# Attention and mixture of experts in one program: expert blocks in the attention's buffers, two of them between its last steps, and another order of a step's pieces

## The chip, the cores and the metric

The kernel runs on one core of one Trainium2 chip. The core has five engines that run side by side and in order, each its own list of instructions: TensorE (PE, with its weight loads PEld), VectorE (DVE), ScalarE (ACT), GpSimd (POOL) and SyncE (SP), which here issues most DMAs. The metric is the device time in microseconds of the slowest core, of which there is one; smaller is better.

## The reference

```python
x = hidden                                            # (4, 1024, 256), float32
x = x + layernorm(attention(layernorm(x)))
x = x + layernorm(experts(layernorm(x)))

def attention(x):                                     # 16 heads of 16
    q, k, v = heads(x @ Wq + bq), heads(x @ Wk + bk), heads(x @ Wv + bv)
    pos_k = heads(rel_embeddings @ Wk + bk)           # 128 buckets
    scores = (q @ k.T + take(q @ pos_k.T, c2p_pos) + take(k @ pos_k.T, p2c_pos).T) / sqrt(48)
    out = softmax(scores) @ v @ Wo + bo + x
    return layernorm(out) * ln_scale + ln_bias

def experts(x):                                       # 8 experts, 256 -> 1024 -> 256
    e = argmax(softmax(x @ Wr + br))
    out = 0
    for i in range(8):                                # an expert sees zeros for the rows of others
        out = out + relu((x * (e == i)) @ W1[i] + b1[i]) @ W2[i] + b2[i]
    return out
```

What an expert gives for a row of zeros is the same for all rows, so the kernel adds it once as a constant (`dh`), and each row needs only its own expert.

## The kernel before, in words

Everything is float32. All work after the setup is issued under a manual schedule: an engine's instructions run in the order in which the program's functions are called, and waits come only from data and from buffers that must come free. So the order of calls in the loop over steps is the schedule.

**Attention.** There are 128 steps `u`, one for each batch element (4), group of four heads (4) and tile of 128 queries (8), and 4 more to finish. Step u does the first pass of its tile: `turn_x` and `first_x` put position terms and scores near the diagonal into four PSUM banks, `near_x` (L523, L527) drains them on VectorE into a `kept` tile and takes maxima, `first_y` (L540, L547, L548) does the same for the other keys, and GpSimd takes the maxima off `kept` (L552). `tables(u+3)` (L435, L441) computes position tables three steps ahead, which go to HBM and come back skewed (`skewed`) into `qpos` and `kpos` tiles; `mend` (L460) repairs their edges. Beside it runs the second pass over the four tiles before, a block of 512 queries, two key tiles in a step: `turn_near` (L576) and `keys` (L598) build transposed scores, ScalarE takes exp (L605) into a `pt` tile, and `sums` (L615) multiplies it by the values into the one bank `pv`. After the eighth key tile ScalarE copies `pv` to `sv`, and `divide` (L634, L639) in the next step turns it round. There are seven other banks (`unit`), handed out in turn. A step with s = u mod 4 equal to 0 also has `maxima` and `add_maxima` (L558, L565), which bring the row maxima of the block's four tiles into q.

**The queue.** When the last head group of 512 rows is divided, `finish` puts the rest of these rows' work into a list, two row tiles an item: `turn` (L690), `out_proj` (L703, L707), `scale` (L716, L717), `scaled`, `residual` (L90, L732), `again`, `logits0`, `logits` (L756), `logits2` (L767), `choose` and `place`, then the scatter of row numbers into the experts' lists, which goes into a second list, `late`. `slot()` takes one item of the first list, `one_late()` one of the second. A step has three slots, the four steps behind the last tile five.

**Experts.** Rows are worked in 39 blocks of 128 rows of one expert. 17 of them hold only rows of the first three batch elements and are planned before the last one is done. A block is `gather` (an indirect DMA), `measure` and `center` (layernorm, L90), `turn_in` (L965, L967), `layer1` (L977; relu L985 on ScalarE and L987 on VectorE in turn), `layer2` (L994, L997) and `close` (layernorm, residual, scatter to the output, L1007). `weights(i)` loads 2 MB for a block through SP's queue (L936, L938), two blocks ahead, into pools of their own that are opened when the attention's pools are closed. The loop over blocks calls, in this order: center(i+1), layer1(i), close(i-1), slot, weights(i+2), turn_in(i+1), slot, measure(i+2), start, layer2(i), slot, slot.

Of the kernel before, what the change touches and what calls it, by code (L numbers as in the profile page):

```python
# [47 lines left out]
def tile_layer(  # L48
# [49 lines left out]
    with ExitStack() as ax:  # L98
# [267 lines left out]
        inner = ax.enter_context(ExitStack())  # L366
        qkp = inner.enter_context(tc.tile_pool(name="qkp", bufs=2))
        vp = inner.enter_context(tc.tile_pool(name="vp", bufs=NG + 1))
        ring = inner.enter_context(tc.tile_pool(name="ring", bufs=4))
        ptp = inner.enter_context(tc.tile_pool(name="ptp", bufs=2))  # L370
# [303 lines left out]
        queue, late = [], []  # L674

        def finish(b, hf):
# [6 lines left out]
            rs, keep_ = {}, {}  # L683

            def turn(t):
                pm = unit()
                for n in range(2):
                    for k in range(KC):
                        at = (n * KC + k) * P
                        nc.tensor.transpose(pm[:, at : at + P], ctx_[:, t_0 + t + n, k * P : (k + 1) * P], ident)  # L690
                cT = two.tile([P, 512], F32, name="cT", tag="sv")
                nc.scalar.copy(cT, pm)
                xr = xin.tile([P, 2, C], F32, name="xr", tag="xt")
                r0 = (b * NT + t_0 + t) * P
                nc.sync.dma_start(out=xr, in_=xrh[r0 : r0 + 2 * P, :].rearrange("(t p) c -> p t c", p=P))
                keep_[t] = cT, xr

            def out_proj(t):
                cT, xr = keep_.pop(t)
# [19 lines left out]
            def scaled(t):  # L719
# [4 lines left out]
                xt = xin.tile([P, 2, C], F32, name="xt")  # L724
                nc.sync.dma_start(out=xt, in_=x_t[b][:, t_0 + t : t_0 + t + 2, :])
                keep_[t] = xt

            def residual(t):
                xt = keep_.pop(t)
                for n in range(2):  # L730
                    normalize(o[:, t + n, :], o[:, t + n, :], agg[1], rs[1], t + n)
                nc.gpsimd.tensor_tensor(o[:, t : t + 2, :], o[:, t : t + 2, :], xt, ALU.add)  # L732
                r0 = (b * NT + t_0 + t) * P
# [44 lines left out]
            def choose():  # L778

# [35 lines left out]
            pairs = range(0, HT, 2)  # L815
            for t in pairs:
                queue.append((turn, t))
                if t:
                    queue.append((out_proj, t - 2))
            queue.append((out_proj, HT - 2))  # L820
# [13 lines left out]
            for t in range(HT):  # L834
                queue.append((late.append, (scatter, t)))
# [79 lines left out]

        live = {}

# [9 lines left out]
        def weights(i):  # L927
# [5 lines left out]
            dr = v["dr"] = e_p[0].tile([P, C], F32, name="dr", bufs=4)  # L933
            nc.sync.dma_start(out=dr, in_=dh[e].to_broadcast([P, C]))
            w1 = v["w1"] = w_p[0].tile([P, KC, FF], F32, name="w1")
            nc.sync.dma_start(out=w1, in_=w1_d[e].rearrange("o (k p) f -> p (o k) f", p=P))  # L936
            w2 = v["w2"] = w_p[0].tile([P, NFC, C], F32, name="w2")
            nc.sync.dma_start(out=w2, in_=w2_d[e].rearrange("o (f p) c -> p (o f) c", p=P))  # L938

        def gather(i):  # L940

            v = live[i]
            x = v["x"] = e_p[0].tile([P, C], F32, name="x", bufs=7)
# [11 lines left out]
        def center(i):  # L955
            v = live[i]
            xn = v["xn"] = e_p[0].tile([P, C], F32, name="xn", bufs=2)
            normalize(xn, v["x"], *v["agg"], 0)

        def turn_in(i):  # L960
# [5 lines left out]
            x2T = v["x2T"] = e_p[0].tile([P, KC, TB], F32, name="x2T", bufs=2)  # L966
            nc.scalar.copy(x2T.rearrange("p k t -> p (k t)"), pm[:, :C])  # L967

        def layer1(i):
            v = live[i]  # L970
            h = v["h"] = e_p[0].tile([P, NFC, TB], F32, name="h", bufs=2)
            for f0 in range(0, NFC, 4):
                ph = unit()
                for j in range(4):
                    f = f0 + j
                    for kc in range(KC):
                        nc.tensor.matmul(  # L977
                            ph[:, j * TB : (j + 1) * TB], lhsT=v["w1"][:, kc, f * P : (f + 1) * P], rhs=v["x2T"][:, kc, :],
                            start=(kc == 0), stop=(kc == KC - 1),
                        )  # L980
                for j in range(4):
                    f = f0 + j
                    hp, b = ph[:, j * TB : (j + 1) * TB], v["b1s"][:, f : f + 1]
                    if j % 2 == 0:
                        nc.scalar.activation(h[:, f, :], hp, AF.Relu, bias=b)  # L985
                    else:
                        nc.vector.tensor_scalar(h[:, f, :], hp, b, 0.0, ALU.add, ALU.max)  # L987

        def layer2(i):
# [3 lines left out]
            for f in range(NFC):  # L993
                nc.tensor.matmul(py, lhsT=v["h"][:, f, :], rhs=v["w2"][:, f, :], start=(f == 0), stop=(f == NFC - 1))  # L994
            agg = small.tile([P, NT, 2], F32, name="agg")
            ys = v["ys"] = e_p[0].tile([P, C], F32, name="ys", bufs=3)
# [4 lines left out]
        def close(i):  # L1001

            v = live.pop(i)
            y = e_p[0].tile([P, C], F32, name="y", bufs=4)
# [76 lines left out]

        for u in range(NU + QB):
# [3 lines left out]
            if s == 0:  # L1086
                slot()
                ahead(u, load, 0)
                if one:
                    turn_x(u)  # L1090
                if one:
                    first_x(u)
                if two_:
                    pm = maxima(blk)
                if one:
                    near_x(u, 0, 2)
# [12 lines left out]
                if tails:  # L1109
                    divide(*tails.pop(0))  # L1110
                ahead(u, prep1, 1)
                extras(u)
# [8 lines left out]
                slot()  # L1121
                if two_:
# [5 lines left out]
                if u + 1 < NU:  # L1128
                    mend(u + 1, 0)
                if one:  # L1130
                    first_y(u)
                one_late()
            else:
                if two_:
                    turn_near(*where(blk, 2 * s))
                if two_:
                    keys(blk, 2 * s)
                if one:
                    turn_x(u)
                if one:  # L1140
                    first_x(u)
                if one:
                    near_x(u, 0, GH)
                ahead(u, load, 0)
# [8 lines left out]
                slot()  # L1153
                sums(0)
                if two_:
                    turn_near(*where(blk, 2 * s + 1))
                if two_:
# [5 lines left out]
                if tails:  # L1163
                    divide(*tails.pop(0))
# [118 lines left out]
```

## Time and profile before

| what | value |
|---|---|
| time, median of 3 runs | 2078.43 us (2071.1 to 2079.08) |
| profiled execution, its own time | 2073.61 us |
| its span | 2071.9 us |
| TensorE, VectorE, ScalarE, GpSimd busy | 94%, 69%, 47%, 27% |
| HBM read and written | 316.85 and 153.83 MB |

The span runs from the first to the last instruction; the execution's own time has 1.7 us more around it. All shares and durations in the text come from that one execution. In rows of instructions, `[4.53 <-DVE xn L90]` says that the engine sat idle 4.53 us just before and what released it. TensorE's records are pipelined and their ends are modelled, so a busy TensorE need not be at its peak; a float32 matmul shows as more than one record.

### The profile page before, as it was taken

To read this page: it belongs to the slowest core of one execution; us is meant where nothing else is said; L and a number is where in the kernel's file an instruction comes from. 1 tells how busy PE (TensorE), PEld (TensorE's weight loads), DVE (VectorE), ACT (ScalarE), POOL (GpSimd) and SP (SyncE) were. 2 spreads that over 40 slices of the span, in tenths; PEclk is the share of its full clock that TensorE was granted. 3 is DMA by queue.
4 is the path that set the end of the run, shared out by engine and by line. 5 is a ranking of instruction groups with operands and counts; after the bars stand their busy time and mean duration, and the time that the engine had idled before them with its cause. 6 is when DMAs were issued, how large, how long until landed. Compare 5 with 4: busy or idle time off the path is not lost.

```text
span 2071.9 us, 43363 instructions
## 1 busy us (share of the span) xinstructions
PE 1951.6 (94%) x15727; PEld 1191.7 (58%) x15727; DVE 1431.5 (69%) x4765; ACT 965.4 (47%) x1916; POOL 569.8 (27%) x966
## 2 busy tenths in 40 slices
PE   7799999999999999999999999999999998899996
PEld 4455555555555555555555555555555555789996
DVE  5567676868677668686767686877786765665654
ACT  1245555554555555554545555545465543122221
POOL 2112212322222213222222222222322122444442
PEclk9899999999999999999999999999999998999999
DMA  5777777766566678665667786666677735799994
GB/s 153 232 253 249 252 248 245 261 216 212 184 220 210 206 229 256 214 212 188 215 208 224 230 258 214 208 196 206 213 216 215 246 118 172 236 332 347 350 337 142
DMA packets 387657, 472.60 MB, mean 228 GB/s; under 512 B 27711, under 2 KB 374931, under 8 KB 387444
## 3 DMA queue, kind: packets, MB, share of 16 engines
q1 hardware_dynamic: 382676, 460.49, 69.4%
q0 software_dynamic: 4768, 9.33, 1.5%
q8 instruction: 125, 2.05, 0.4%
q14 instruction: 88, 0.72, 0.1%
HBM read 316.85 MB, written 153.83 MB: 227 GB/s over the span
## 4 chain that ended last, share of the span: by engine, by line
PE 69%; DVE 15%; DMA 8%; issue 3%; ACT 2%; POOL 1%; SPq 0%; POOLq 0%; DVEq 0%; ACTq 0%
PE pv L615 9%; PE u L598 8%; PE u L540 7%; PE u L576 6%; PE u L491 6%; PE u L387 5%; PE u L435 5%; PE u L994 5%; PE u L507 5%; PE u L977 5%; DVE mx L547 3%; DMA shift<-stage 2%; DVE qpos L460 2%; DMA qpos<-shift 2%; DVE kept L523 2%
## 5 line engine op out<-in xcount | busy, mean ns | idle before, releaser
L605 ACT ACTIVATE pt<-u 128x512 f32<-128x512 f32 x1024 | 529.8, 608 | 268.2 <-PE u L598 262.4
L547 DVE TENSOR_REDUCE mx<-u 128x1 f32<-128x512 f32 x512 | 317.5, 682 | 197.8 <-PE u L540 197.8
L552 POOL TENSOR_SCALAR kept<-kept,m 128x384 f32<-128x384 f32 (+1 forms) x512 | 291.9, 586 | 524.5 <-DVE m L548 357.9
L441 ACT COPY stage<-u 128x512 f32<-128x512 f32 x512 | 263.1, 604 | 320.0 <-issue 179.2
L523 DVE CUSTOM_DVE_ANT_0 kept<-u,qpos 128x384 f32<-128x384 f32 (+1 forms) x512 | 263.4, 515 | 137.6 <-PE u L507 137.4
L615 PE MATMUL pv<-pt,v 128*24 128x512 f32 x2048 | 274.6, 605 | 0.0
L576 PE MATMUL u<-ident,kept 128*128 128x128 f32 x1408 | 200.7, 282 | 34.5 <-DVE mx L527 22.5
L576 PEld LDWEIGHTS u<-ident,kept 128*128 128x128 f32 x1408 | 153.0, 142 | 137.7 <-issue 39.0
L443 POOL COPY ends<-stage 128x8 f32<-128x8 f32 x128 | 26.5, 207 | 655.8 <-ACT stage L441 655.8
L491 PE MATMUL u<-ident,kpos 128*128 128x128 f32 x1408 | 194.3, 285 | 11.2 <-DMA kpos<-shift 6.3
L491 PEld LDWEIGHTS u<-ident,kpos 128*128 128x128 f32 x1408 | 155.0, 143 | 78.9 <-DVE mx L547 21.4
L460 DVE SCALAR_TENSOR_TENSOR qpos<-mask,ends,qpos 128x128 f32<-128x128 f32 x448 | 177.3, 456 | 23.8 <-DMA qpos<-shift 23.8
L985 ACT ACTIVATE h<-u,b1s 128x128 f32<-128x128 f32 x156 | 55.6, 367 | 236.7 <-issue 140.4
L527 DVE TENSOR_REDUCE mx<-u 128x1 f32<-128x128 f32 (+1 forms) x512 | 162.6, 318 | 0.0
L540 PE MATMUL u<-k_hi,q 32*128 32x512 f32 (+3 forms) x768 | 155.2, 509 | 7.2 <-ACT pt L605 5.7
L460 DVE SCALAR_TENSOR_TENSOR kpos<-mask,ends,kpos 128x128 f32<-128x128 f32 x448 | 131.9, 355 | 28.7 <-DMA kpos<-shift 28.7
L977 PEld LDWEIGHTS u<-x2T,w 128*128 128x128 f32 x1248 | 147.5, 195 | 2.6 <-ACT x2T L967 0.9
L977 PE MATMUL u<-x2T,w 128*128 128x128 f32 x1248 | 148.4, 278 | 0.5 <-ACT x2T L967 0.5
L994 PE MATMUL u<-w,h 128*128 128x256 f32 x624 | 145.3, 387 | 0.0
L507 PE MATMUL u<-k,q 32*128 32x384 f32 (+2 forms) x1792 | 137.0, 415 | 0.0
L540 PEld LDWEIGHTS u<-k_hi,q 32*128 32x128 f32 x768 | 83.5, 184 | 77.1 <-ACT pt L605 50.7
L994 PEld LDWEIGHTS u<-w,h 128*128 128x128 f32 x624 | 118.6, 195 | 15.4
(198 smaller groups left out, 2405.0 us busy)
## 6 DMA issues: line engine op xcount, KB each, us to landing
shift<-stage SPq DMA_DIRECT2D x256, 510.0 KB
kpos<-shift SPq DMA_DIRECT2D x128, 768.0 KB
qpos<-shift SPq DMA_DIRECT2D x128, 768.0 KB
w<-in_L_ffn_W_dram SPq DMA_DIRECT2D x78, 1024.0 KB
xt<-_attn_hidden_states_dram SPq DMA_DIRECT2D x32, 256.0 KB
w<-in_L_ffn_W_dram SPq DMA_DIRECT2D x16, 512.0 KB
dr<-dh SPq DMA_DIRECT2D x39, 128.0 KB
xrh<-xt SPq DMA_DIRECT2D x16, 256.0 KB
```

Source lines behind the costliest of these rows:

```text
L441: nc.scalar.copy(st[:, h].rearrange("p m w -> p (m w)"), us[h][:, : 2 * (TW + 1)])
L460: nc.vector.scalar_tensor_tensor(w, mask[:, m, :], ends[u][:, m, h : h + 1], w, ALU.mult, ALU.add)
L491: nc.tensor.matmul(us[h][:, (c - a) * P : (c - a + 1) * P], lhsT=near[u - i + c, 1][:, h, at : at + P], rhs=ident, start=(c == a), stop=Fa ...
L523: nc.vector.tensor_tensor_reduce(out=sn[:, h, w0 : w0 + nw], in0=us[h][:, :nw], in1=near[u, 0][:, h, w0 : w0 + nw], scale=1.0, scalar=-3.0 ...
L540: nc.tensor.matmul(us[h][:, at : at + (c1 - c0) * P], lhsT=proj[n, "q"][r : r + HP, i * P : (i + 1) * P], rhs=proj[n, "k_hi" if small_k el ...
L547: nc.vector.tensor_reduce(mx[:, h, 2:3], us[h], AX.X, ALU.max)
L552: nc.gpsimd.tensor_scalar(w, w, m4[:, i % QB, j : j + 1], 1.0, ALU.add, ALU.mult)
L576: nc.tensor.matmul(us[h][:, (t - t0) * P : (t - t0 + 1) * P], lhsT=kept[n * NT + t][:, h, at : at + P], rhs=ident, start=(t == a), stop=Fa ...
L605: nc.scalar.activation(pt[:, h, :], us[h], AF.Exp)
L615: nc.tensor.matmul(pv[h * HP : h * HP + VW, :], lhsT=vals[b][g][:, c, h, :], rhs=pt[:, h, :], start=first, stop=last)
L977: nc.tensor.matmul(ph[:, j * TB : (j + 1) * TB], lhsT=v["w1"][:, kc, f * P : (f + 1) * P], rhs=v["x2T"][:, kc, :], start=(kc == 0), stop=( ...
L994: nc.tensor.matmul(py, lhsT=v["h"][:, f, :], rhs=v["w2"][:, f, :], start=(f == 0), stop=(f == NFC - 1))
```

## The change

The expert blocks no longer have pools of their own. A block's weights lie in attention tiles that are out of use by then, in a round of four: the position stage and the transposed input, four `kpos` tiles, four `kept` tiles, two `pt` tiles; its small tiles lie in the position table `tab`, in the projection weights, in value tiles and in q and k tiles. So the attention's pools stay open, and weights are loaded three blocks ahead, where a tile is smaller in halves. Blocks 0 and 1, and the first pieces of block 2, are called at fixed places in the steps from 125 to 131 (`EARLY`), and the loop over blocks starts at 2. It has one slot more per block. All eight relus of a block go to ScalarE.

In `finish`, the rows that out_proj and residual add are loaded by items of their own (`fetch`), ahead of their use, the stores of the result move from `residual` into `choose`, and all out_proj items follow all turn items. The scatters enter `late` by one item instead of four. For the last half both loads are issued in step 129 (`fetch_last`).

In a step with s = 0 the first slot, which stood before `turn_x`, stands behind `divide`; `mend(u+1, 0)` moves ahead of the second `turn_near`, and `one_late` behind `maxima`. In the other steps the slot that stood behind `tables` and `skewed` stands between the first `keys` and `turn_x`, `divide` stands ahead of the first `keys`, and `one_late` takes the place of that slot.

```diff
@@ pools of the attention
-        inner = ax.enter_context(ExitStack())
-        qkp = inner.enter_context(tc.tile_pool(name="qkp", bufs=2))
+        qkp = ax.enter_context(tc.tile_pool(name="qkp", bufs=2))
...
@@ finish
             def turn(t):
...
-                xr = xin.tile([P, 2, C], F32, name="xr", tag="xt")
-                nc.sync.dma_start(out=xr, in_=xrh[...])
...
+            queue.append((fetch, b, hf, "xrh"))
             for t in pairs:
                 queue.append((turn, t))
-                if t:
-                    queue.append((out_proj, t - 2))
-            queue.append((out_proj, HT - 2))
+            for t in pairs:
+                queue.append((out_proj, t))
+            queue.append((fetch, b, hf, "x"))
...
-            for t in range(HT):
-                queue.append((late.append, (scatter, t)))
+            queue.append((late.extend, [(scatter, t) for t in range(HT)]))
@@ weights, gather, center, turn_in, layer1
+            row2 = vp.tile([P, NT, GH, VW], F32, name="v").rearrange("p t h e -> p (t h e)")
+            v["dr"], v["ys"] = (row2[:, j * C : (j + 1) * C] for j in range(2))
...
-            w1 = v["w1"] = w_p[0].tile([P, KC, FF], F32, name="w1")
-            w2 = v["w2"] = w_p[0].tile([P, NFC, C], F32, name="w2")
+            if i % 4 == 0:
+                tiles = (stg.tile(...), xts.tile(...))
+            elif i % 4 == 3:
+                tiles = [ptp.tile([P, GH, 512], F32, name="pt") ... for _ in range(2)]
+            else:
+                tiles = [ring.tile([P, GH, WIN], F32, name=("kpos", "kept")[i % 4 - 1], bufs=(4, 5)[i % 4 - 1]) ... for _ in range(4)]
...
-            x = v["x"] = e_p[0].tile([P, C], F32, name="x", bufs=7)
+            x = v["x"] = spare[:, i % 6, :]
...
-                    if j % 2 == 0:
-                        nc.scalar.activation(h[:, f, :], hp, AF.Relu, bias=b)
-                    else:
-                        nc.vector.tensor_scalar(h[:, f, :], hp, b, 0.0, ALU.add, ALU.max)
+                    nc.scalar.activation(h[:, f, :], hp, AF.Relu, bias=b)
@@ steps
+        EARLY = {
+            (NU - 3, 1): [(weights, 0)],
+            (NU - 2, 2): [(start, 2)],
+            (NU - 1, 2): [(measure, 0), (measure, 1), (center, 0)],
+            (NU, 0): [(weights, 1)],
+            (NU, 1): [(turn_in, 0)],
+            (NU, 2): [(center, 1), (layer1, 0)],
+            (NU + 1, 0): [(fetch_last,)],
+            (NU + 1, 1): [(turn_in, 1), (measure, 2), (start, 4)],
+            (NU + 1, 2): [(layer2, 0)],
+            (NU + 2, 1): [(center, 2)],
+            (NU + 2, 2): [(layer1, 1), (close, 0)],
+            (NU + 3, 0): [(weights, 2)],
+            (NU + 3, 1): [(turn_in, 2), (measure, 3), (start, 5)],
+            (NU + 3, 2): [(layer2, 1)],
+        }
...
             if s == 0:
-                slot()
-                ahead(u, load, 0)
...
                 if tails:
                     divide(*tails.pop(0))
+                slot()
                 ahead(u, prep1, 1)
+                ahead(u, load, 0)
...
                 slot()
+                early(u, 1)
+                if u + 1 < NU:
+                    mend(u + 1, 0)
+                early(u, 0)
                 if two_:
                     turn_near(*where(blk, 2 * s + 1))
...
             else:
                 if two_:
                     turn_near(*where(blk, 2 * s))
+                if tails:
+                    divide(*tails.pop(0))
                 if two_:
                     keys(blk, 2 * s)
+                slot()
                 if one:
                     turn_x(u)
...
                 if 0 < u + 2 < NU:
                     skewed(u + 2, 0)
-                slot()
+                one_late()
                 sums(0)
...
-        inner.close()
-        w_p = [ax.enter_context(tc.tile_pool(name="w_p", bufs=3))]
-        e_p = [ax.enter_context(tc.tile_pool(name="e_p", bufs=2))]
...
+        weights(3)
+        weights(4)
-        for i in range(NB):
+        for i in range(2, NB):
...
-                weights(i + 2)
+                weights(i + 3)
...
             start(i + 4)
+            slot()
             layer2(i)
```

## The prediction

> **What bounds the kernel now.** I read the page's busy shares first, then the busy time by stage, then the waits of TensorE, and last the order of time where those waits lie.
>
> ```profile
> PE 1951.6 (94%) x15727; PEld 1191.7 (58%) x15727; DVE 1431.5 (69%) x4765; ACT 965.4 (47%) x1916; POOL 569.8 (27%) x966
> PEclk9899999999999999999999999999999998999999
> ```
>
> TensorE is busy 1951.6 of 2071.9 us, so about 120 us are idle in all, and a change that removes no matmul can only win from those and from the dips of the clock. Where they lie is told by stages:
>
> ```profile
> 1194.90:1291.70 96.80, 94.49 (x825) 51.07 (x824) 71.34 (x233) 56.59 (x109) 28.37 (x52) 1.00 0.75 239
> 1405.40:1517.70 112.30, 105.75 (x861) 58.62 (x861) 83.69 (x269) 56.54 (x109) 30.33 (x49) 0.97 0.66 207
> 1699.80:1762.67 62.87, 53.81 (x343) 35.13 (x339) 29.16 (x104) 23.37 (x49) 15.48 (x17) 0.88 0.46 151
> 1762.67:1843.26 80.59, 70.63 (x453) 64.65 (x452) 56.28 (x202) 15.63 (x44) 37.34 (x43) 0.94 0.89 274
> 1843.26:2041.65 198.39, 196.63 (x1351) 184.64 (x1350) 117.27 (x378) 45.59 (x135) 86.21 (x108) 1.00 1.03 338
> ```
>
> Columns: stretch, its length, then PE, PEld, DVE, ACT, POOL busy, granted clock, DMA share, GB/s. Row 1 is eight attention steps with an empty queue: 97.6% busy at full clock. Row 2 is eight steps that also work off a finished half's queue. Row 3 is the last four attention steps and blocks 0 and 1, clock 0.88. Row 4 is blocks 2 to 9, among which the last half is finished. Row 5 is 27 blocks at 7.35 us. TensorE sets the pace everywhere; rows 2 to 4 are where it is held up. Its waits in the third stretch, and those of steps 32 to 111:
>
> ```profile
> PE u L756 <- DVE xn L90: 4.5, 1, 4.5
> PE u L965 <- DVE xn L90: 2.8, 1, 2.8
> ...
> PE u L576 <- DVE mx L527: 17.9, 16, 3.0
> PE u L576 <- DVE mx L547: 6.0, 6, 2.1
> ```
>
> In the tail it waits for VectorE's normalised rows, in attention for VectorE to drain banks (L527 is near_x).
>
> **Part 1: two blocks between the last steps, no hole before block 2.** Before, from the start of block 31's first turn_near (1699.80) to layer1 of block 2 (1762.67) is 62.9 us. At the durations that the same groups have where the clock is 1.00 (pv 0.96 for four heads and one key tile, four 512-wide key products 1.14, out_proj 1.99, 12 transposes 1.53 and so on) the attention tail adds to 29.5 us, each block to 3.7 (layer1) + 3.4 (layer2) + 0.25 (turn_in), and the remaining queue items to about 2: 46 us. The other 17 us are holes and a slow clock:
>
> ```profile
> 1730.30 1.11 PE L756 MATMUL u<-ident,xn 128*128 128x128 f32 x4 [4.53 <-DVE xn L90]
> 1742.70 0.69 PE L965 MATMUL u<-ident,xn 128*128 128x128 f32 x2 [2.85 <-DVE xn L90]
> 1743.89 6.29 PE L977 MATMUL u<-x2T,w 128*128 128x128 f32 x32 [0.51 <-ACT x2T L967]
> ...
> 1802.11 0.76 PE L756 MATMUL u<-ident,xn 128*128 128x128 f32 x4 [1.89 <-DVE xn L90]
> ...
> 1803.02 5.30 PE L994 MATMUL u<-w,h 128*128 128x256 f32 x16
> ```
>
> Layer1 takes 3.73 us elsewhere and 6.29 here; layer2 5.30 instead of 3.62 behind a hole of only 1.89. The Trainium skill (TensorE: Matmul & The Clock Gate, Why this matters for your kernels) puts the fall to half clock at idle gaps over about 3 us. By that rule only the 4.53 gap would cost clock; by these rows gaps of 1.9 and 2.9 each cost 1.7 to 2.6 more. I follow the rows: every hole counts nearly double.
>
> What stays: logits of half (3,0) needs the serial chain out_proj, scale, scaled, residual, again, logits0, which took 17.0 us (1713.4 to 1730.4). The new order puts layer2(0) and layer1(1) into it, so that TensorE has about 17.3 us of work between out_proj's end and that logits (two pairs of pv 3.8, transposes and key products 6.1, layer2 3.4, layer1 3.7, turn_in 0.25). But the blocks put their own VectorE work into the chain: ys with its statistics 1.2, center 0.4, close 0.83, and 0.8 waiting for layer2(0), so the chain becomes about 20.3. A hole of 3 us is left, with the clock about 5.5; the sv copy before the last divide keeps 0.7. Part 1 brings 17 - 6.2 = about 11 us; between 6 (a second hole as large) and 16 (none).
>
> Its other instructions are costed at nothing, each with its cover. ScalarE gets 16 relus (5.9 us) and three copies beside eight groups of exp (16.5 us) in some 45 us. POOL gets three gathers (1.0 us each) after step 126's masks; it is 22% busy. Measuring and centring at the end of step 127 put 1.9 us of VectorE before add_maxima, of which about 0.6 shows, since the first turn_near waits for POOL's L552 (2 us) anyway. On SP's queue weights(0) is issued in step 125 and waits for the last stage tile (step 124); behind it stand the last skewed loads, which wait for the same shift store. weights(1) and weights(2) wait for kpos and kept tiles, with only fetches behind. DMA share is 0.48 in 1650 to 1700 and 0.31 in 1700 to 1750. Uncovered, one late 1 MB transfer would cost 3 us at the 349 GB/s of 1740 to 1762.
>
> **Part 2: the queue's items in the blocks.** Row 4 has 8 blocks (8 x 7.25 = 58.0) and 8.7 us of queue matmuls: 66.7, so 14 us lost. The largest hole, 3.72 us (and layer2 6.05 behind it), comes from a 3.27 us wait of VectorE for xr. The last half's xrh and x are now fetched from step 129, so this goes: 4 to 6 us. Five slots per block instead of four make VectorE denser. Scale twice and scaled twice and a residual are about 7 us, beside 3.2 of the block itself; before it was 6.2 beside 4.6 with the four relus. So the other holes stay. Taken: 3 us; ends -2 and 8.
>
> **Part 3: relus on ScalarE.** L985 on ACT is 367 ns, L987 on DVE 349 ns. Eight in a row are 2.9 us of ScalarE in a 7.25 us block, and they lose the alternation (each waited 0.42 for the other engine), while VectorE loses 1.4 us. The Trainium skill (ScalarE: Activation LUTs, Rules for kernel authors) speaks against it: relu on VectorE, up to about three times faster in bf16. At 3 x 349 ns, eight would take 8.4 us, over the block's 7.25: 37 x 1.1 = 43 us lost. The f32 rows show 1.05 times, so I take the rows. The last relu is done about 1.7 us after layer1, and layer2 needs it 3.4 us after. Row 5 can win at most 198.4 - 27 x 7.25 = 2.6; taken 1, ends 0 and 2.6. More and smaller weight DMAs (two or four per block, 118 in all instead of 78) add two issues of about 0.6 us on SP in half of the blocks; SP waits for buffers there (L938 39.4 us), and no matmul waits for w. One block more of prefetch therefore buys nothing.
>
> **Part 4: the order of a step.** With an empty queue the engines' orders are unchanged but for some masks, so row 1 stays. The 48 steps with a full queue (six stretches, 672 us, 642 busy) change in two ways. First, a step with s = 0 loses the item ahead of near_x:
>
> ```profile
> 631.73 0.41 DVE L78 BATCH_NORM_STATS2 st<-o 128x6 f32<-128x256 f32 x1
> ...
> 633.00 0.55 DVE L523 CUSTOM_DVE_ANT_0 kept<-u,qpos 128x384 f32<-128x384 f32 x1
> ...
> 633.91 0.41 PE L576 MATMUL u<-ident,kept 128*128 128x128 f32 x2 [2.60 <-DVE mx L527]
> ```
>
> Those statistics (1.3 us) hold near_x, and TensorE's transposes wait 2.60. The item now stands behind divide, where VectorE was idle 6.96 us (step 36). Two such steps per batch element, about 1.3 to 3 us each: 4 us. Second, in the other steps one item of three moves from behind tables to ahead of turn_x, so on VectorE ahead of near_x, where TensorE has about 5 us of work against VectorE's 2.65 (draining first_y) + 1.1 (mask) + items, and 7 us after it. Where the item is scale (1.9 us) near_x comes late and tables wait; the fetch item, which has no VectorE work, takes up part of it (step 34 comes out equal, step 42 1.9 us late, step 43 0.7). I count 2.3 us per batch element back. Three batch elements: 3 x (4 - 2.3) = about 5 us won; ends -15 and 12. One store later (at choose) and the earlier loads lift waits on SP (L735 16.2 us) that end on nobody's path.
>
> **Sum.** 11 + 3 + 1 + 5 = 20 us on the profiled execution: span 2071.9 to about 2052. That execution took 2073.61, 4.8 below the median of the three runs (2071.1 to 2079.08). Against the median: 2078.4 - 20 = 2058.4. A measurement of this kernel can tell about 0.5%, 10.4 us, from no change.
>
> **Rivals.** *Slower: the item ahead of near_x.* Per batch element the heavy items there are out_proj twice, scale twice, scaled and four light ones, 11.3 us of VectorE; 34 us in all. Fully exposed, with half as much again in clock, 51; less the 15 of the other parts and the 12 that the s = 0 steps win: +24, 2102. It decides from about 27 us, just over half. For it: L435 already waits for near_x (0.79 and 0.65). Against: work moved forward is missing later, and VectorE is busy only 76% of these stretches. *No change:* the tail is bound by chains, not by missing work: 17 + 3 us of VectorE chain plus blocks' reads of late ys, so block 2 starts no more than 4 us earlier, and part 4 nets to nothing: 2073. For it: ScalarE and VectorE each carry blocks and attention in order. Against: each is busy less than half of that stretch. *All holes go:* 16 + 9 + 2 + 10 = 37: 2041. That the change does not do what it says is excluded: in its instruction order on TensorE both blocks stand between the key products.
>
> **Chances.** Forecast 0.60 (2048 to 2068), all holes 0.10, no change 0.18, slower 0.12. Faster by over 0.5%: 0.70; within: 0.18; slower: 0.12. The range leaves out the slower case and a little of the ends: 2040 to 2078.
>
> **What would show it.** From the first turn_near of block 31 to layer1 of block 2 about 52 us instead of 62.9, clock over 0.94, one hole before the logits transposes. Block 3's out_proj without a wait for xrh. Eight ACT relus back to back; 7.25 to 7.3 us per block. Steps 36 and 44 with waits on L527 near 1.3 instead of 2.6. Wrong: a matmul waiting for weights, tables waiting over 1.5 us for near_x in most full steps, or the steps' stretch of row 2 over 112 us.

## The result: slower, and the profile after

The changed kernel took 2099.18 us in the median of four runs (2095.39 to 2104.28), the kernel before 2074.76 beside it: ratio 1.0121, 95% interval 1.009 to 1.0152. That is 24 us slower where 20 us less were forecast. The profiled execution took 2104.28 us with a span of 2102.6, the slowest of the four. Lines of the profile after carry the numbers of the new file: in the attention each is one lower than before (near_x L527 is now L526), in the blocks some 30 higher.

The page of the kernel after, its busy shares and the granted clock:

```profile
PE 1968.4 (94%) x15727; PEld 1201.2 (57%) x15727; DVE 1384.4 (66%) x4609; ACT 999.8 (48%) x2072; POOL 568.3 (27%) x966
PEclk8789999999989999999899999999899999999998
```

The number of matmuls is the same, and TensorE is 17 us busier: its work got slower, not more. Where the clock fell is told by the stretches that answer to the five of before (stretch, length, PE, PEld, DVE, ACT, POOL busy, granted clock, DMA share, GB/s):

```profile
1223.20:1319.60 96.40, 94.51 (x826) 51.09 (x825) 71.30 (x233) 56.63 (x109) 28.40 (x52) 1.00 0.75 241
1431.90:1553.00 121.10, 111.77 (x863) 61.30 (x862) 84.23 (x272) 56.38 (x109) 30.10 (x50) 0.92 0.68 192
1739.31:1789.73 50.42, 45.04 (x323) 30.50 (x319) 22.59 (x72) 24.78 (x56) 13.99 (x17) 0.97 0.33 106
1789.73:1867.33 77.60, 70.76 (x473) 65.02 (x472) 49.27 (x189) 23.27 (x77) 35.57 (x40) 0.98 1.01 305
1867.33:2074.00 206.67, 198.44 (x1352) 184.88 (x1350) 82.88 (x270) 69.38 (x243) 88.37 (x111) 1.00 0.98 316
```

Rows 1, 3 and 4 came out as forecast: steps with an empty queue are unchanged (96.8 to 96.4), the tail is shorter (62.9 to 50.4), blocks 2 to 9 are shorter (80.6 to 77.6). Row 2, eight steps with a full queue, went from 112.3 to 121.1, and its clock from 0.97 to 0.92; the prediction had named a row 2 over 112 us as a sign of being wrong. From profile to profile the whole balance is: set-up and the first 32 steps +2.9 us, the three stretches with a full queue (24 steps each) +38.5, the empty steps between them -1.1, step 120 to block 2 -13.3, blocks 2 to 9 -3.0, blocks 10 to 36 +8.3, the end -1.7; together +30.6 of the span's 30.7.

TensorE's waits in the kernel after from step 32 to 1560 us, in step 112 (us in total, times, longest):

```profile
PE u L434 <- DVE mx L526: 15.8, 9, 2.5
PE u L575 <- DVE mx L526: 12.4, 22, 1.8
PE u L539 <- DVE o L713: 10.9, 3, 4.5
PE u L575 <- DVE mx L546: 10.1, 4, 7.5
```

Up to the end of step 111 the wait on near_x at the near transposes fell from 17.9 to 10.2, and tables (L434) wait for near_x instead: that exchange was in the prediction. The lower two rows are what it did not have. There are few such waits and they are long, and each has a time and a place. Step 40 of the kernel after, in order of time (start, duration, engine, line; in brackets the idle time before and its releaser):

```profile
574.13 1.20 POOL L817 DMA_INDIRECT lists<-ids,si  x1 [0.67 <-issue]
577.46 1.16 SPq L682 DMA_DIRECT2D xt<-xrh  x2
...
583.23 1.00 POOL L817 DMA_INDIRECT lists<-ids,si  x1 [4.56 <-DMA lists<-ids,si]
...
592.67 0.69 DVE L713 TENSOR_TENSOR o<-u,xt 128x512 f32<-128x512 f32 x1 [5.98 <-DMA xt<-xrh]
...
593.42 2.06 PE L539 MATMUL u<-k,q 32*128 32x512 f32 x4 [4.54 <-DVE o L713]
```

SP issued the 512 KB of xrh at 577.46; out_proj's drain on VectorE got them 15 us later, and first_y waited behind it. Two list scatters (L817), those of steps 39 and 40, lie around the fetch. Step 40 took 26.55 us where it took 14.78, of which step 41 gave 4 back. In step 48 the same happens to the skewed loads:

```profile
692.00 1.09 POOL L817 DMA_INDIRECT lists<-ids,si  x1 [0.57 <-issue]
694.50 0.37 SPq L452 DMA_DIRECT2D kpos<-shift  x1
694.97 0.50 SPq L452 DMA_DIRECT2D qpos<-shift  x1
...
700.94 1.00 POOL L817 DMA_INDIRECT lists<-ids,si  x1 [4.27 <-DMA lists<-ids,si]
703.98 1.14 DVE L459 SCALAR_TENSOR_TENSOR kpos<-mask,ends,kpos 128x128 f32<-128x128 f32 x4 [4.38 <-DMA kpos<-shift]
...
710.97 1.14 DVE L459 SCALAR_TENSOR_TENSOR qpos<-mask,ends,qpos 128x128 f32<-128x128 f32 x4 [5.85 <-DMA qpos<-shift]
...
712.76 0.90 PE L575 MATMUL u<-ident,kept 128*128 128x128 f32 x3 [7.50 <-DVE mx L546]
```

TensorE stands 7.5 us at the end of a chain that begins with a load: kpos, issued at 694.50, is there for VectorE 9.5 us later. In the kernel before, the load comes first and the scatter behind it, and VectorE has kpos after 5.4 us:

```profile
683.67 0.37 SPq L453 DMA_DIRECT2D kpos<-shift  x1
686.02 1.08 POOL L810 DMA_INDIRECT lists<-ids,si  x1 [0.17 <-issue]
689.09 1.14 DVE L460 SCALAR_TENSOR_TENSOR kpos<-mask,ends,kpos 128x128 f32<-128x128 f32 x4 [0.28 <-DMA kpos<-shift]
```

What the DMA engines did from 690 to 712 in the kernel after, in 40 slices, with the time from issue to landing of the second of these scatters, and then from 676 to 698 in the kernel before:

```profile
GB/s 56 0 0 0 258 330 345 321 351 290 37 184 290 89 61 31 25 56 39 64 28 6 257 397 394 399 420 334 349 291 78 87 65 52 50 63 83 184 204 124
...
lists<-ids,si POOLq DMA_INDIRECT x2, 10.7
```

```profile
GB/s 369 377 402 397 276 3 8 3 0 0 308 321 351 349 345 235 87 176 310 221 307 397 391 402 388 172 47 0 0 0 284 334 269 35 217 189 295 213 63 0
```

In the kernel after, twice, for some 4 to 5 us beginning about 5 us behind a scatter (692.00 is slice 4, 700.94 slice 20), the rate falls from about 300 to 400 GB/s to under 90. In the kernel before the rate behind the scatter (686.02, slice 19) is 220 to 400 until the transfers end. A scatter writes 128 rows of 4 bytes, 512 bytes in all. The change moved the call of `one_late`, which issues them, from the end of a step to its middle (behind maxima where s = 0, behind the skewed loads elsewhere). SP issues the skewed loads only when it has waited for the store to `shift`, so POOL issues a scatter that is called behind them ahead of them (692.00 and 694.50 above). Before, the first two scatters of a half came 13.4 to 14.7 us apart and no two in these steps closer than 10.6, and the step's loads were issued ahead of them; in the kernel after the first two come 7.6 to 9.1 us apart.

### The profile page after: what moved, and what is told of

Same layout as the page of the kernel before. It is cut to its first block, busy times and chain, and to the rows that moved or that the text cites. A ratio compares the mean times of both kernels' runs of the same rounds, so it can differ in the third digit from the quotient of the medians.

```text
span 2102.6 us, 43491 instructions
## 1 busy us (share of the span) xinstructions
PE 1968.4 (94%) x15727; PEld 1201.2 (57%) x15727; DVE 1384.4 (66%) x4609; ACT 999.8 (48%) x2072; POOL 568.3 (27%) x966
## 4 chain that ended last, share of the span: by engine, by line
PE 69%; DVE 12%; DMA 12%; issue 3%; ACT 2%; POOL 2%; SPq 1%; POOLq 0%; DVEq 0%; ACTq 0%
PE pv L614 10%; PE u L597 8%; PE u L539 8%; PE u L575 7%; PE u L490 6%; PE u L434 6%; PE u L386 5%; PE u L506 5%; PE u L1023 4%; DVE mx L546 3%; PE u L1009 3%; DMA it<-lists 2%; DMA xt<-xrh 2%; DMA shift<-stage 2%; DMA kpos<-shift 2%
## 5 line engine op out<-in xcount | busy, mean ns | idle before, releaser
L526 DVE TENSOR_REDUCE mx<-u 128x1 f32<-128x128 f32 (+1 forms) x512 | 163.1, 318 | 0.0
L434 PE MATMUL u<-tab,q 32*128 32x256 f32 x1024 | 115.4, 434 | 19.9 <-DVE mx L526 17.2
L86 POOL TENSOR_TENSOR rs<-ve,half 128x1 f32<-128x1 f32 (+2 forms) x118 | 81.8, 694 | 178.5 <-DVE ve L85 168.8
L597 PE MATMUL u<-q,k_hi 32*128 32x512 f32 (+3 forms) x1024 | 126.7, 522 | 3.5 <-DVE q L564 1.9
L434 PEld LDWEIGHTS u<-tab,q 32*128 32x128 f32 x1024 | 54.2, 188 | 121.4 <-issue 106.0
L539 PE MATMUL u<-k,q 32*128 32x512 f32 (+3 forms) x640 | 105.0, 518 | 10.9 <-DVE o L713 10.9
```

Of the source, the lines that this page charges most:

```text
L434: nc.tensor.matmul(us[h][:, m * (TW + 1) : (m + 1) * (TW + 1)], lhsT=proj[n, src][r : r + HP, ts], rhs=tab[r : r + HP, g, m, :], start=Tru ...
L539: nc.tensor.matmul(us[h][:, at : at + (c1 - c0) * P], lhsT=proj[n, "q"][r : r + HP, i * P : (i + 1) * P], rhs=proj[n, "k_hi" if small_k el ...
L597: nc.tensor.matmul(us[h][:, (f0 - t0) * P : (f1 - t0) * P], lhsT=proj[n, "k_hi" if small_k else "k"][r : r + HP, c * P : (c + 1) * P], rhs ...
```

## The experiments

Three theories stood at the start. S: the scatters' new place costs the time. A: the queue item ahead of near_x costs it (the prediction's slower rival). F: the fetch of xrh is too close to its use. Ratios are to the kernel before, run beside each on the same chip.

**The scatters back at the end of a step** (late_end): in the changed kernel

```
                 if two_:
                     pm = maxima(blk)
-                one_late()
...
                     first_y(u)
+                one_late()
                 early(u, 2)
...  (and in the same way in the other three steps of four)
```

> The changed kernel with one_late put back at the end of a step, as in the kernel before; everything else as changed. Theory S (a scatter into the lists, 128 rows of 4 bytes, holds up the DMA engines for some 8 us, and the new places put it ahead of the skewed loads and two of them close together): steps 40 and 48 of a batch element lose their waits for xrh, kpos and qpos, three times about 7 and 6 us: 2099 - 39 = about 2060. Theory A (the queue's item ahead of near_x makes VectorE late): nothing changes, 2099. Theory F (the two xrh loads of the second half are issued one step ahead of out_proj, behind other loads): step 48 may get better, step 40 keeps its wait for xrh: about 2085.

2065.84 us against 2066.95: ratio 0.9986 (0.9965 to 1.0007). Against the change's 1.0121 that is 1.35% or 28 us. Step 40 in the profile of late_end:

```profile
572.67 2.04 SPq L682 DMA_DIRECT2D xt<-xrh  x2
573.90 1.20 POOL L817 DMA_INDIRECT lists<-ids,si  x1 [0.18 <-issue]
582.45 0.69 DVE L713 TENSOR_TENSOR o<-u,xt 128x512 f32<-128x512 f32 x1 [4.16 <-DMA xt<-xrh]
582.81 1.51 PE L539 MATMUL u<-k,q 32*128 32x512 f32 x8
```

VectorE still waits 4.16 us for xrh, as the fetch stands as close to its use as before, but the transfer takes under 10 us instead of 15 and first_y does not wait. So F is not the cause by itself. TensorE's waits in late_end from step 32 to 1560 us:

```profile
PE u L434 <- DVE mx L526: 16.2, 9, 2.5
PE u L575 <- DVE mx L526: 12.4, 20, 2.0
...
PE u L575 <- DVE mx L546: 2.5, 3, 1.3
```

The waits for near_x are as large as in the changed kernel (15.8 and 12.4 us), so they are not what it lost by; those behind out_proj (10.9 us) and behind the late loads (10.1) are gone or small. The three stretches with a full queue take 961.3 us instead of 998.1.

**The scatters alone, in the kernel before** (before_late): the step order of before, with `one_late` at the change's places and nothing else changed.

> The kernel before with one thing changed: one_late at the two places of the changed kernel (behind maxima; behind the skewed loads). Theory S: slower by what the skewed loads lose, three times 6 us or more: 2093 to 2110. Theory A or F: no change, 2075.

2094.02 us, ratio 1.0139 (1.0107 to 1.0171): 27 us slower from a move of 24 small DMA calls. Both directions agree. In its profile the three full stretches take 978.3 us, against 959.6 and 963.1 in the two profiles of before, so 15 to 19 of the 27 us are seen there; where the others lie was not measured.

**The item ahead of near_x put back** (mid_slot), alone and together with the scatters (late_mid):

```
-                slot()
                 if one:
                     turn_x(u)
...
                     skewed(u + 2, 0)
+                slot()
```

> The changed kernel with the slot between keys and turn_x put back behind tables and skewed; one_late stays in its new place. Theory A: the waits of tables for near_x in steps 41 to 46 go, three times about 5 to 7 us: 2099 - 18 = 2081, and if all of the loss were there, 2065. Theory S: those few us at most (L434 waited 2.48 and 1.38 in two steps), the waits of steps 40 and 48 stay: 2085 to 2095.

> Both undone: one_late at the end of a step and the slot behind tables. Theory S and A together: 2060 less what the slot brings, 2045 to 2055. If the slot ahead of turn_x did good on balance (step 36 lost 4 us less), this is slower than the kernel with one_late alone put back.

mid_slot 1.0162 (1.0138 to 1.0186), no better than the change; late_mid 0.9983 (0.9969 to 0.9997), the same as late_end and, at 2063.37 us, above the 2045 to 2055 that S and A together would have given. Theory A falls: its price is not to be seen beside the scatters, nor without them.

**One scatter of four put back** (s0_back): only the call in the steps with s = 0.

> The changed kernel with only the scatter of the steps with s = 0 put back to the end of the step; the other three of four stay where the change put them. Theory S1 (the loss is made by the s = 0 scatter, which comes 9 us after the one before it where the others are 14 us apart, and lies ahead of fetches): nearly all of the 33 us comes back, ratio to before 0.998 to 1.003, and steps 40 to 47 take about 110 us instead of 118.0. Rival S2 (each scatter that stands in the middle of a step collides with that step's loads): only about a quarter comes back, ratio about 1.010, steps 40 to 47 about 116 us.

Ratio 1.0039 (1.0015 to 1.0063): of the 1.35% between the change and late_end, 0.82 come back, some 60%. The times themselves (2084.56 us, against 2099.18 and 2065.84) give 44%, and the three full stretches 41% (983.0 us, against 998.1 and 961.3); the kernel before was slower on this chip than beside late_end (2077 and 2067), which moves the ratio. Neither theory had that: the scatters of the s = 0 place cost more than a quarter, and the other three cost as well. Steps 40 to 47 of the first batch element took 118.4 us where S1 expected about 110 and S2 116, no less than in the changed kernel (118.0). In its profile step 40 still took 24.2 us: a scatter at 570.13, the fetch at 573.66 behind it, and first_y 2.17 us late again. So it seems to be a scatter ahead of a load that is needed soon that counts, in whichever step.

**How a scatter holds things up** (dose): POOL waits for the scatter before (4.56 and 4.27 us above), and what stands behind it on POOL waits too; or the rows hold up the other transfers. One kernel with the change's order tries both, by batch element; it was profiled in one execution:

```
             def scatter(t):
+                if b == 0:
+                    return
+                r = P if b == 1 else 16
                 nc.gpsimd.indirect_dma_start(
-                    out=lists[:, :], ...(ap=keep_["si"][:, t : t + 1], axis=0),
+                    out=(apart[t] if b == 1 else lists)[:, :], ...(ap=keep_["si"][:r, t : t + 1], axis=0),
```

> The changed kernel with its scatters varied by batch element, in their new places: left out for the first; for the second all 128 rows of each, but the four of a half go to four tables of their own, so that none waits on POOL for the one before; for the third only 16 of the 128 rows of each. It leaves out most of the lists (the padding then points at row 0). Times of steps 32 to 55, 64 to 87 and 96 to 119, which are 333.5, 331.1 and 333.5 us in the changed kernel and about 320 in the kernel before. Theory D (the 128 rows of a scatter hold up the loads of the other queues): about 319, 330 and 321. Theory P (POOL stands still until the scatter before has landed, and with it masks and gathers): about 319, 320 and 321. If neither (the places cost by something else than the scatters): 330 in all three.

The stretches of the kernel after, then those of dose:

```profile
462.50:796.00 333.50, 308.46 (x2561) 173.04 (x2560) 236.35 (x773) 167.23 (x321) 81.24 (x146) 0.97 0.70 202
892.10:1223.20 331.10, 312.39 (x2562) 173.28 (x2561) 234.96 (x773) 167.16 (x321) 81.35 (x146) 0.96 0.68 204
1319.60:1653.10 333.50, 315.19 (x2563) 174.60 (x2562) 242.19 (x798) 167.19 (x321) 80.84 (x146) 0.96 0.68 202
```

```profile
462.90:781.50 318.60, 305.89 (x2561) 170.14 (x2560) 236.42 (x773) 167.24 (x321) 73.13 (x138) 0.98 0.66 212
877.80:1213.20 335.40, 314.02 (x2562) 176.09 (x2561) 236.34 (x773) 167.27 (x321) 81.53 (x146) 0.95 0.67 201
1309.20:1633.00 323.80, 309.03 (x2563) 171.88 (x2562) 241.93 (x798) 167.33 (x321) 80.02 (x146) 0.97 0.65 208
```

Without scatters 318.6, which is 15 us less. With all rows to four tables 335.4: POOL no longer waits for the scatter before (0.16 us in step 72, 3.00 in the changed kernel), and nothing is won; it is 4 us more, with the first two scatters of a half now 5 us apart. With 16 rows of 128, 323.8: nearly all of the loss in this batch element is gone (late_end takes 323.0 there). So the rows hold up the loads, and POOL's own wait is a bystander. VectorE's waits of dose in its second batch element (985 to 1075 us; its lines stand one higher than in the kernel after) name the loads again, with 5.9 and 2.7 us in the changed kernel and none in dose's first batch element:

```profile
DVE o L714 <- DMA xt<-xrh: 5.1, 1, 5.1
DVE kpos L460 <- DMA kpos<-shift: 2.8, 1, 2.8
```

The records of single DMA packets show it most directly. A packet of SP's queue takes 0.05 us in the median. Packets over 1 us are 56, 19 and 40 in the three full stretches of before, 23, 21 and 23 in late_end, but 200, 147 and 145 in the changed kernel, the longest 4.2 us, and nine in ten of these start within 8 us behind a scatter's own packets. In dose they are 33 without scatters, 162 with all rows and 25 with 16 rows.

**The same doses at the ends of steps** (dose_late, made from late_mid_begin below):

> late_mid_begin with the same three doses as in the kernel dose: no scatters in the first batch element, full scatters to four tables of their own in the second, 16 rows of each in the third; it leaves out most of the lists (the padding then points at row 0). Steps 32 to 55, 64 to 87 and 96 to 119 take 323.9, 317.6 and 324.7 us with all scatters (late_mid_begin's second profile). If a scatter at the end of a step is free: 321 to 324, 317 and 324 again. If it costs there too, by a third of what it costs in the middle: about 318, 318 and 319.

315.8, 322.7 and 323.7 us, again in one execution. The first batch element is 5 to 9 us under the six other profiles of that attention order (320.5 to 325.1); the third is where theirs are (321.3 to 325.0), the second 3 to 6 us above (317.2 to 319.6). So a scatter at the end of a step costs between nothing and a few microseconds for each half, no steady amount; the two answers offered do not cover it.

**The rest of the step's order** (order_old): the changed kernel with the steps before 125 in the order of before.

> The changed kernel with the steps before 125 in the order of the kernel before (scatters at the end of steps too); the blocks between the last steps, the queue's own order, the fetches and the relus stay as changed. Theory O (the rest of the new order of a step costs about 8 us of attention, and with the scatters put back it eats most of the 12 us that the tail won): ratio to before 0.994, and below that of late_end and late_mid (0.998). Rival (the order of a step is worth nothing either way, and the tail's gain is lost in set-up or in the blocks): 0.998 again.

Ratio 1.0079 (1.0049 to 1.0109), 1% slower than late_end. The theory falls: with the new queue it is the old order of a step that costs, 988.1 us in the three full stretches against 961.3. A part of it can be named: with the two fetch items in the queue `place` comes two slots later, in old steps at step 39, where TensorE waits 1.88 and 0.86 us for its inputs, and step 39 takes 14.19 us (8.15 in before). This step and its like make 17 of the 27 us; what makes the others was not measured.

**A second profile of before** (before_again).

> The kernel before, unchanged, for a second profile of it beside the experiments. If the first profile (step 120 at 1612.7 us) is typical of it, the attention up to step 120 is no faster in before than in late_end (1609.4) and late_mid (1615.4), and the tail's 12 us must show in the medians; if the order of a step costs about 8 us, step 120 starts at about 1605 here. Tail (step 120 to layer1 of block 2) 150 us and blocks from there to the end 309 us in both.

Step 120 at 1617.7 us, and the span 2082.0, longer than in the first profile (2071.9). From step 120 to layer1 of block 2 it took 147.8 us (150.0 in the first), and blocks 10 to 36 took 207.7 us instead of 198.4. So the attention up to step 120 is no faster in before than in late_end (1609.4), and that last stretch varies from execution to execution by more than the change moved it, and the +8.3 us above say nothing.

**The lists loaded earlier** (late_mid_begin): late_mid, with the list of a block loaded one block earlier, ahead of that block's weights on SP's queue; then both once more side by side.

```
                     start(i + 4)
+                begins(i + 5)
                 weights(i + 3)
```

> late_mid (scatters and the item before turn_x put back) with the load of each block's list issued one block earlier, ahead of that block's weights on SP's queue. Theory G (in the blocks the list's load stands behind more weight issues than before, the gather waits for it on POOL, the rsqrt behind the gather comes late, and center and turn_in with it): the gathers' waits for the list go from 34 us to under 5, and from layer1 of block 10 to layer1 of block 37 it takes about 196.5 us instead of 200.8; ratio to before about 0.996 where late_mid had 0.998. Rival (the blocks are held by the weights' transfers): stays at 200 to 201 us and 0.998.

> late_mid once more, beside late_mid_begin on one chip. Theory G (the earlier load of the lists is worth about 4 us): ratio about 0.996. Rival C (the two ratios 0.998 and 0.994 differ by the chip on which the kernel before ran, whose own median was 2067 in one call and 2077 in the other): within 0.001 of late_mid_begin's.

> late_mid_begin once more, beside late_mid and no_early. Theory G: 0.994, about 4 us below late_mid. Rival C: the same as late_mid within 2 us, wherever both lie.

First 0.9937 (0.9909 to 0.9964); side by side 0.9963 (0.9939 to 0.9987) against late_mid's 0.9984 (0.9959 to 1.0009): 2059.69 and 2065.92 us. The intervals overlap, so the medians alone do not settle theory G, and its 4 us are an estimate. The profiles show what it did. POOL's waits in blocks 10 to 36, first late_mid's second profile, then late_mid_begin's:

```profile
POOL tab L976 <- DMA it<-lists: 43.7, 20, 3.4
```

```profile
POOL rs L86 <- DVE ve L85: 57.1, 23, 3.8
...
POOL tab L976 <- issue: 4.9, 26, 0.2
```

The gathers no longer wait for the list, and POOL waits for VectorE instead, as it should. The stretch took 195.6 us, 27 times 7.245 with nothing lost (199.0 in its other profile), against 200.8 and 203.2 in late_mid's two. With it the kernel beats both the kernel before and the changed one.

**The blocks after the attention** (no_early): late_mid_begin, with what `EARLY` holds run behind the last step, apart from fetch_last.

> late_mid_begin with the weights, gathers and blocks 0 and 1 issued after the attention's last step instead of between its last steps; the fetch of the last half's tiles stays early, all else as there. If part 1 is worth what the profiles of the changed kernels show (62.9 to about 50.4 us from the first turn_near of block 31 to layer1 of block 2), this is slower than late_mid_begin by 12 us or more: ratio 1.000 or above. If the tail's gain is given back in the blocks behind it: within 4 us of late_mid_begin.

2068.94 us, ratio 0.9998 (0.998 to 1.0016): 9 us over late_mid_begin beside it, where 12 or more were expected. From step 120 to layer1 of block 2 it took 146.3 us against 137.5.

**The relus in turn again** (relu_alt): late_mid_begin with

```
-                    nc.scalar.activation(h[:, f, :], hp, AF.Relu, bias=b)
+                    if j % 2 == 0:
+                        nc.scalar.activation(h[:, f, :], hp, AF.Relu, bias=b)
+                    else:
+                        nc.vector.tensor_scalar(h[:, f, :], hp, b, 0.0, ALU.add, ALU.max)
```

> late_mid_begin with the relus of the blocks alternating between ScalarE and VectorE again, as before the change. The prediction's part 3: from layer1 of block 10 to layer1 of block 37 it takes about 1 us more than late_mid_begin (195.6 to 199.0 in its two profiles), which no median can tell; ratio 0.995 plus or minus 0.002. Rival (VectorE's relus hold up measure, center and ys, and eight on ScalarE freed it): blocks 2 to 10 take over 81 us instead of 77.6 and blocks 10 to 37 over 200. Rival on the other side (eight relus in a row are what layer2 waits for): 195.6 exactly, and layer1 to layer1 of blocks 2 to 10 below 77.

2081.66 us, ratio 1.007 (1.0047 to 1.0094), where late_mid_begin had 0.9937 and 0.9963: by these ratios some 22 to 27 us slower, where 1 us was expected. Blocks 2 to 9 and 10 to 36, first relu_alt, then late_mid_begin's second profile:

```profile
1764.61:1857.31 92.70, 77.34 (x472) 69.63 (x471) 60.85 (x221) 15.97 (x45) 35.15 (x40) 0.91 0.85 258
1857.31:2055.97 198.66, 196.07 (x1351) 184.62 (x1350) 117.07 (x378) 46.37 (x135) 88.67 (x110) 1.00 1.00 327
```

```profile
1753.25:1830.92 77.67, 70.86 (x473) 65.02 (x472) 49.55 (x189) 23.25 (x77) 35.79 (x41) 0.98 1.01 307
1830.92:2026.53 195.61, 195.61 (x1351) 184.46 (x1350) 81.93 (x270) 68.62 (x243) 88.03 (x110) 1.00 1.00 333
```

Of it 15.0 us lie in blocks 2 to 9, 6.7 in the attention's tail (144.2 us from step 120 instead of 137.5), and about 3 or less in the blocks without a queue. TensorE's holes in the tail and in block 5 of relu_alt show the way:

```profile
1751.44 0.87 PE L761 MATMUL u<-ident,xn 128*128 128x128 f32 x3 [5.76 <-DVE xn L90]
...
1801.17 0.41 PE L997 MATMUL u<-ident,tab 128*128 128x128 f32 x2 [3.65 <-DVE tab L90]
```

VectorE's relus are in its order among the queue's items and the block's center. In blocks 2 to 9 they take 10.8 us themselves (32 at 349 ns), and VectorE stands another 11.6 us waiting for ScalarE's relus in turn with them. The normalisations for logits and turn_in stand behind them.

## Why the prediction was wrong

**The step that failed** is in part 4: "The 48 steps with a full queue (six stretches, 672 us, 642 busy) change in two ways." They change in three. The sum priced the two moves of queue items, put DMAs aside with "the earlier loads lift waits on SP (L735 16.2 us) that end on nobody's path", and left the third move out. `one_late` stands in the diff: it moved from the end of a step to its middle, so that its scatters came ahead of loads that they had followed, and they were costed at nothing without a word on what covers them. Moved back, they give 28 us; moved alone in before, they cost 27; left out of one batch element, 15 us in it.

The forecast of 20 by its terms:

- **Part 1, 11 us: right.** The stretch went from 62.9 to 50.4 us (52 forecast). One main hole before the logits transposes (2.38 us; 3 forecast), the clock 0.97 (over 0.94 forecast), the sv copy's 0.78. A second hole of 1.72 us at the near keys was forecast as 0.6. By no_early it is worth 9 us of the median.

```profile
1741.69 0.93 PE L597 MATMUL u<-q,k_hi 32*128 32x384 f32 x8 [1.72 <-DVE q L564]
...
1779.33 0.67 PE L761 MATMUL u<-ident,xn 128*128 128x128 f32 x4 [2.38 <-DVE xn L90]
```

- **Part 2, 3 us: right in its stretch** (80.6 to 77.6, 77.6 to 78.6 in late_end, late_mid and late_mid_begin; 79.4 in the second profile of before), and out_proj of the last half no longer waits for xrh. But the "two issues of about 0.6 us on SP" of part 3 were weighed only by whether a matmul waits for weights. What waits behind them on SP is the load of the next list, and behind that POOL's gather, the rsqrt, center and turn_in; the runs put it at some 4 us, with intervals that overlap.
- **Part 3, 1 us: mis-sized by some twenty times.** It was read from row 5, the blocks without a queue, where it is indeed about 3 or less. The prediction's own part 2 has the reason why that is the wrong row: five items per block on VectorE. Eight relus on ScalarE are what makes room for them. It adds nothing to the sum, since parts 1 and 2 were counted with VectorE already free of relus: with half of the relus back, step 120 to block 10 takes 236.9 us, and 230.5 in before, so the gains of parts 1 and 2 are gone. The Trainium skill's advice to use VectorE for relu, up to about three times faster in bf16 (ScalarE: Activation LUTs, Rules for kernel authors), was rightly set aside here: relu_alt follows it with only half of the relus and loses. The prediction's price for following it, 37 x 1.1 us, is 41 and not 43; nothing rests on that.
- **Part 4, 5 us: about nothing.** In late_end, where the scatters are back at the ends of steps, step 36 and its like in the other batch elements won 2.8 to 4.1 us, and step 42 and its like lost 1.0 to 3.7 where 1.9 was forecast. Over the three full stretches late_end needs 961.3 us against 959.6 and 963.1 in the two profiles of before. The slower rival priced the item ahead of near_x at 34 to 51 us; mid_slot and late_mid show no cost of it.

The slower rival's figure (2102) lies near the measured time by luck: the cost that it names is not the one that was paid. Neither it nor the range held a collision of transfers, though the DMA engines were busy 0.66 of row 2.

**Left open.** In their profiles the tail of late_end and late_mid (136.6 to 139.0 us from step 120 to block 2) is 9 to 13 us shorter than in before (150.0 and 147.8), and their medians are 1 to 3.6 us below it. late_mid_begin gets 9.5 and 14 us. Some four of the missing microseconds are the lists' loads. For the rest: before's own median moved from 2065 to 2077 us from chip to chip while late_mid stayed at 2063 to 2066, and no profile of before comes from a chip on which it was fast. Which stretch of it was shorter there was not measured. How a scatter's 128 rows make other packets slow is open too: the runs show that they do, not by what.

## What to carry to other kernels

A call that moves in a diff is a step of the change even if it is a tiny DMA on an idle engine: ask which transfers are under way behind it, and who waits for the first of them. Put scatters of many small rows behind the loads of a stage, not ahead of them. Keeping them apart may help too (here 10.6 us or more in the kernels without the loss), but the distance was not varied alone. And price a shift of work between engines in the stretch where the receiving or the freed engine is dense, not in the one where it has room.

## What had not been expected of the hardware

An indirect scatter of 128 rows of 4 bytes takes about 1 us of POOL and lands 5.4 to 11.2 us after its issue in the changed kernel. Beside loads, 4 to 5 us of that pass with the 16 DMA engines moving under 90 GB/s where they had moved 300 to 400, because single packets of SP's queue take up to 4 us instead of 0.05. POOL's queue is not the reason, and hardly the bytes: a scatter's 512 are a third of one 1536-byte packet of the kpos load. With 16 rows of 128 nearly all of the loss went (333.5 to 323.8 us, 323.0 in late_end). Rows and bytes were reduced together, so that it is the number of rows is argued from the size, not shown apart. At eight scatters per batch element a badly placed one costs about 1.9 us (15 us by 8), or 1.1 us by the 27 us of all 24 in before_late.
